# An attention-and-convolution kernel: where the first strip's projection, its normalization and the transposes stand in the order of work

## The chip, the cores and the metric

The kernel runs on one core of a Trainium2 chip. The metric is the device time of one execution in microseconds (us); lower is better. The shown time is the median of three executions. A profile is taken of one further execution, and all durations of single instructions come from that one.

Engines are named as the profile names them: PE is TensorE (matrix products; PEld is its weight load), DVE is VectorE, ACT is ScalarE, POOL is GpSimd, and SP is SyncE, whose queue issues the strip transfers. A line such as L62 is a line of the kernel's file.

## The reference

The input x has 8 images of 384 channels and 64 x 64 pixels, in float32. Two layers are applied, each on a group-normalized input and each with a residual:

```python
x = x + attention(_gn(x))      # layer 0
x = x + conv_layer(_gn(x))     # layer 1
```

- `_gn` normalizes 32 groups of 12 channels over all pixels of an image.
- Layer 0 is a LayerNorm over the channels, a q, k, v product, attention in windows of 8 x 8 pixels, and an output projection (`out @ proj_w + proj_b`). Half of the channels (4 heads of 48) use plain windows, the other half (4 heads) windows shifted by 4 pixels, with a mask. Each window's softmax has a relative position bias.
- Layer 1 is a 1x1 product with `w_in`, a filter in the 8 x 8 Fourier domain (`rfft2`, a product, `irfft2`), a depthwise 3x3 convolution, a gate (`gelu(x1) * x2`), and a 1x1 product with `w_out`.

## The kernel before, in words

**Tiles.** An image is cut into 8 strips of 8 rows, that is 512 tokens with 3 x 128 channels. A strip s of image b has two attention units, one for the plain and one for the shifted windows (br = 0 and 1), numbered w = 16b + 2s + br. Layer 1 of image b needs the group mean and deviation of the whole of layer 0's result x1, so it runs beside the attention of image b+1. It begins with strip 0 at place 16(b+1) + 2; before that come two units in which the attention of the new image has little of layer 1 beside it. The second of them, unit 16(b+1) + 1, is called the short unit here. It runs on PE from the end of one score product (pS) to the first q tile of the next unit.

**One unit on PE.** pS (scores), three tiles of pq (q and k of the next unit, 6 passes each), two tiles of pvv (v), pT (transposes of the softmax weights, `turn`), pA (weights times v, `apply`), and pr (output projection of a finished strip, `project`, three tiles of three passes). The pieces of layer 1 lie between: pt (`mix`), pf (`transform`), pz (`back`) and pw (`finish`).

**The other engines.** DVE does the softmax (e, mx, rc), the residual addition x_add after pr (L624), the statistics of the strip (st, in `keep`), eight of the nine taps of the convolution (zz, L784), and the LayerNorm scaling y. ACT copies q, k, v out of PSUM (qab, kab, kcd, qcd, v), takes exponentials, copies the transposes (eT) and the weighted values (o, L598 to L604), applies the second group norm (xn, `normal_x1`, L653) and copies z from pz. POOL does three copies of y (L451 to L453) and issues the transfers that put o into the layout oT for the projection. The oT of strip 0 has one buffer of its own, since that strip's projection can come only when the shifted windows of strip 7 have wrapped around.

**The second group norm.** `keep` takes the statistics of each strip of x1. When all eight are there, `second_mean` aggregates them (mv_b), PE averages over the groups (pm_b), DVE works out the variance (gs_b, gt_b), PE averages again (pv_b), and `second_std` takes the root on ACT (sd_b) and, on DVE, the reciprocal and the shift (sh, L638 to L645). `normal_x1` of strip 0 needs sh.

**What sets the order.** Each piece is put in a plan by `at(place, piece, ...)` (from about L843 on), where the place is a unit with a fraction. The pieces are issued in order of place. PE's instructions keep exactly this order. For the other engines a scheduler sets the order when the program is built; once built, each engine runs its own list in order. Strip transfers go through SP's queue, each behind a copy of q (`in_dense_work`); five buffers of tag "x" hold strips. PSUM has four "gemm" buffers of one bank and two "att" pairs.

**Empty instructions.** EMPTY (L29 to L33) lists how many empty instructions go between the dense products of each unit. They shift where the borders of PE's instruction blocks of 256 fall.

**The head.** Before the first unit the q, k and v weights are scaled by the LayerNorm's gain, and the mean over channels is taken off them (`centre` on ACT and PE, `take_off` on DVE, tile pc). The biases come from the tile pb. DVE also takes the statistics of the first image. Strip 0 is then normalized, its row sums `ln_sums` and the spread `rs_first` give the scale of y, and the first pq can start.

Of the kernel before, what the change touches and what calls it, by code (L numbers as in the profile page):

```python
# [18 lines left out]
NS = SW // WS  # L19
# [6 lines left out]
C_ID, C_ONES, C_GRP, C_FWD, C_INV, C_MASK = 0, 128, 256, 384, 512, 640  # L26
C_PICK = C_MASK + 3 * 64
N_CONST = C_PICK + 2
EMPTY = (128, 0, 0, 96, 52, 0, 0, 98, 11, 124, 11, 124, 3, 124, 11, 124, 11, 45, 43, 124, 52, 123, 11, 124,  # L29
         11, 124, 11, 124, 3, 124, 11, 124, 11, 45, 43, 124, 52, 123, 11, 124, 11, 124, 11, 124, 3, 124, 11, 124,  # L30
         11, 45, 43, 124, 52, 123, 11, 124, 11, 124, 11, 124, 3, 124, 11, 124, 11, 45, 43, 124, 52, 123, 11, 124,
         11, 124, 11, 124, 3, 124, 11, 124, 11, 45, 43, 124, 52, 123, 11, 124, 11, 124, 11, 124, 3, 124, 11, 124,
         11, 45, 43, 124, 52, 123, 11, 124, 11, 124, 11, 124, 11, 0, 0, 115)  # L33

STATS_AT = 2.16, 4.16, 5.16, 6.16, 7.16, 8.16, 9.16, 10.16

# [2 lines left out]
def block_kernel(ctx: ExitStack, tc: tile.TileContext, out, x, consts, fsel, wqk, wv, bqk, bv,  # L39
                 wp, bp, lng, lnb, rpb1, rpb2, w_in, w_dw, w_out, filt):  # L40
    nc = tc.nc
# [8 lines left out]
    def psum(name):  # L50
        return ps.tile([P, ST], F32, tag="gemm", name=name)

    def psum2(name):

        return ps.tile([P, 2, ST], F32, tag="att", bufs=2, name=name)
# [16 lines left out]
    def strip(tag, bufs, name):  # L72
        return sb.tile([P, KC, ST], F32, tag=tag, bufs=bufs, name=name)
# [72 lines left out]
    for j, to, n, t, hp, of in blocks:  # L146
        nc.gpsimd.dma_start(out=bqk_sb[to:to + n].rearrange("p (b j) -> p b j", b=2)[:, :, j],
                            in_=bqk[of:of + n, 4 * t:4 * t + 4].rearrange("p (b i) -> p b i", b=2)[:, :, hp])
# [19 lines left out]
    for br, tab in ((0, rpb1), (1, rpb2)):  # L168
        raw = sb.tile([P, 2, 64], F32, tag="t2", bufs=3, name=f"rpb_raw{br}")
        raw_bias.append(raw)  # L170
        for h in range(4):
            half = slice(h % 2 * 64, h % 2 * 64 + 64)
            for y2 in range(WS):
                nc.gpsimd.dma_start(
                    out=raw[half, h // 2, y2 * WS:(y2 + 1) * WS],
                    in_=bass.AP(tab.tensor, h * 225 + y2 * 15, [[15, 8], [1, 8], [1, 8]]),
# [25 lines left out]
    means, biases = {}, {}  # L202

    def all_biases():
        if not biases:
            biases["all"] = psum("pb")
        return biases["all"]

    def centre(w, *key):
        for k in range(KC):  # L210
            nc.scalar.activation(w[:, k], w[:, k], AF.Copy, scale=lng_sb[:, k:k + 1])
        pc = psum("pc")
        for k in range(KC):
            matmul(pc[:, 0:C], ones_c, w[:, k], start=(k == 0), stop=(k == KC - 1))
        means[key] = w, pc
# [83 lines left out]
    def at(place, piece, *args):  # L299
        plan.append((place, len(plan), piece, args))  # L300

    xs, ys, y2s, qks, vs, os_, ots, x1s, zs = ({} for _ in range(9))
# [10 lines left out]
    gs0, gs1, st0s, st1s, x1d = ({} for _ in range(5))  # L313
# [9 lines left out]
    def in_dense_work(i):  # L323


        if zs.get("gate"):
            behind(i, zs["gate"], mybir.DependencyClass.Sync, "transfer in dense work")
# [4 lines left out]
    def load(b, s, what):  # L332

        if b == 0 and (what == "stats" or what == "norm" and s < 3):
            xs[b, s, what] = first_x[s]
            return
        if what == "mix" and s == 0:
            xs[b, s, what] = xs.pop((b, s, "add"))
            return
        t = xs[b, s, what] = strip("x", 5, f"x_{what}_{b}_{s}")  # L340
        src = x1d[b][s] if what in ("mix", "finish") else rows_of(x[b], s)
        in_dense_work(nc.sync.dma_start(out=t, in_=src))
# [289 lines left out]
        strip_stats(st1s[b], s, xs[b, s, "add"])  # L632

    def store(b, s):
        in_dense_work(nc.sync.dma_start(out=x1d[b][s], in_=xs[b, s, "add"] if s == 0 else xs.pop((b, s, "add"))))


    def second_mean(b):  # L638
# [208 lines left out]
    for b in range(B):  # L847
        first = 2 * NS * b

        for s in range(NS):  # L850
            u = first - 16 + STATS_AT[s] if b else -10 + 0.1 * s
            at(u, load, b, s, "stats")
            at(u + (0.5 if b else 0.05), input_stats, b, s)
        if b == 0:

            at(-9.99, pack_qk, 0)
            at(-9.98, qk_weights, 0)
            at(-9.97, v_weights)
            at(-9.96, pack_qk, 1)
            at(-9.95, qk_weights, 1)  # L860
            for place, key in ((-9.82, ("qk", 0)), (-9.62, ("v",)), (-9.42, ("qk", 1))):
                at(place, take_off, *key)
            at(-9.26, qk_bias, 0)
            at(-9.26, v_bias)
            at(-9.26, qk_bias, 1)
            at(-2.7, spread_first)
            at(-0.6, position_bias, 0)
            at(-0.4, position_bias, 1)
            at(0.2, out_bias)
            at(0.2, filter_weights)  # L870
        at(first - 4.8 if b else -8, input_mean, b)
        at(first - 4.4 if b else -7.9, input_std, b)
        for s in range(NS):
            u = first + 2 * s

            v = u - 4
            early = 1.75 if b == 0 and s == 1 else 0
            at(v - 0.84 - early, load, b, s, "norm")
            at(v + 0.15 - early, group_normal, b, s)
            at(v + 0.45 - (1.35 if early else 0), ln_square, b, s)  # L880
            if b:
                at(v + 0.985, small_tiles, v + 1)
            at(v + 0.99 - early, ln_sums, b, s)
            at(v + 0.99 if (b, s) != (0, 1) else -2.6, ln_row, b, s)
            at(v + 1.35, ln_scale, b, s)

            if s:
                at(v + 1.50, shifted_half, b, s - 1, 1)
            else:
                at(u - 1.15, shifted_half, b, NS - 1, 1)  # L890
            at(u - 1.2 if s < NS - 1 else v + 1.55, shifted_half, b, s, 0)
            for br in range(2):
                w = u + br
                for t in range(3):
                    at(w - 1 + (0.14, 0.34, 0.55)[t], qk_tile, b, s, br, t)
                for g in range(2):
                    at(w - 1 + ((0.78, 0.86), (0.67, 0.88))[br][g], v_tile, b, s, br, g)
                at(w + 0.05, scores, b, s, br)
                at(w + 0.12, weights, b, s, br)

                at(w + 0.13, exponent, b, s, br)
                at(w + (0.23, 0.26)[br], divide, b, s, br)
                at(w + 0.80, turn, b, s, br)
                at(w + 1.00, apply, b, s, br)
                at(w + 1.07, put, b, s, br)

            if 0 < s < NS - 1:
                places = [u + 3 + f for f in (0.27, 0.45, 0.70)]
            else:
                places = [first + 2 * NS + f + (0.0 if s else 0.24) for f in (0.36, 0.44, 0.52)]  # L910
            at(int(places[0]) - 0.84, load, b, s, "add")
            for m in range(KC):
                at(places[m], project, b, s, m)
            at(places[2] + 0.1, keep, b, s)
            at(int(places[2]) + 1.15, store, b, s)
        first += 2 * NS
        at(first + 1.25, second_mean, b)
        at(first + (1.90 if b < B - 1 else 1.995), second_std, b)
        if b == B - 1:
            at(first + 2, tap_matrices)  # L920
        for s in range(NS):
            u = first + 2 + 2 * s
            at(u - 0.84, load, b, s, "mix")
            at(u + 0.02, normal_x1, b, s)
            for i in range(4):
                at(u + (0.28, 0.45, 0.60, 0.78)[i], mix, b, s, i)
            for j in range(2):
                at(u + (0.995, 1.02)[j], transform, b, s, j)
            if b < B - 1:
                at(u + 1.985, small_tiles, u + 2)  # L930
            at(u + 1.99, back, b, s)
            at(u + 2.08 if b < B - 1 or s < NS - 1 else u + 1.991, borders, b, s)

            for n, m in enumerate((0, 2, 1)):
                for tap in range(1, 6):
                    at(u + (2.62, 3.10, 3.5)[n] + 0.05 * tap + (0.4 if n == 2 and tap > 3 else 0), conv, b, s, m, tap)
                for tap in range(6, 9):
                    at(u + 4.2 + 0.25 * (n * 3 + tap - 6) / 9, conv, b, s, m, tap)
            if (b, s) in on_pool:
                for place, taps in ((2.45, (0, 1)), (2.8, (2, 3)), (3.15, (4, 5)), (4.15, (6, 7)), (4.3, (8,))):  # L940
                    at(u + place, pool_taps, b, s, taps)
            if (b, s) in on_pe:
                at(u + 2.3, conv_taps, b, s)
            at(u + 5.16, load, b, s, "finish")
            at(u + 4.5, gate, b, s)
            at(u + 6.10, finish, b, s)
# [5 lines left out]
    order = [p[2:] for p in sorted(plan, key=lambda p: p[:2])]  # L952
    dense, empty, counts = [], [0] * len(order), list(EMPTY)
    for i, (piece, args) in enumerate(order):
# [116 lines left out]
```

## Time and profile before

| what | value |
|---|---|
| median of 3 executions | 3534.93 us (3534.86 to 3538.03) |
| profiled execution | 3543.4 us |
| its span | 3541.2 us |
| PE busy | 3460.2 us, 98% |
| DVE busy | 3058.8 us, 86% |
| ACT busy | 2538.1 us, 72% |
| POOL busy | 1060.4 us, 30% |
| short unit at the change from image 2 to 3 (from 1230.53 us) | 23.31 us, PE busy 21.45 |
| long unit before it (1190.84 to 1230.53 us) | 39.69 us |
| long unit, stretch of 1191.00 to 1230.53 us: PE, DVE, ACT busy | 39.53, 31.20, 19.26 us |

The share of busy time says which engine has the least idle time over the whole run. The timeline gives start and duration of each group of instructions, and in brackets the idle time of the engine before it with what ended it ("issue" means that nothing which the profile shows was waited for). The waits view adds these brackets up over the run.

### The profile page before, as it was taken

How to read it: one execution, taken by the hardware profiler on the slowest of the kernel's cores; microseconds unless marked ns; L12 is line 12 of the kernel's file. 1: busy time of each engine (PE TensorE's matmuls, PEld its weight loads, DVE VectorE, ACT ScalarE, POOL GpSimd, SP SyncE). 2: the span in 40 equal slices, each digit the busy share in tenths (PEclk: the TensorE clock that was granted, in tenths of full speed). 3: DMA queues.
4: the chain of work that ended last, by engine and by line, in shares of the span. 5: the costliest groups of instructions: out<-in, count | busy, mean ns of one | idle time of the engine just before them, and what ended most of it. 6: DMA issues, size and time to landing. Idle time of an engine off the chain costs nothing.

```text
span 3541.2 us, 93350 instructions
## 1 busy us (share of the span) xinstructions
PE 3460.2 (98%) x36454; PEld 2197.0 (62%) x36454; DVE 3058.8 (86%) x4330; ACT 2538.1 (72%) x4069; POOL 1060.4 (30%) x1688
## 2 busy tenths in 40 slices
PE   7999999999999999999999999999999999999898
PEld 5665666656666666666666666666666666666454
DVE  4766589989998899988999889998899988987987
ACT  4877687768777687776777767777677767776474
POOL 5333223223232233222233223232233223221254
PEclk8999999999999999999999999999999999999999
DMA  4343234333433234333334323433234333323422
GB/s 125 98 143 106 81 107 156 108 107 122 138 130 127 98 110 156 130 106 118 125 128 144 121 89 134 144 112 136 99 118 154 115 107 110 105 99 108 155 108 81
DMA packets 176100, 421.12 MB, mean 119 GB/s; under 512 B 26656, under 2 KB 29243, under 8 KB 175688
## 3 DMA queue, kind: packets, MB, share of 16 engines
q1 hardware_dynamic: 138832, 364.25, 29.5%
q0 software_dynamic: 36416, 50.65, 5.1%
q8 instruction: 315, 5.16, 0.6%
q14 instruction: 97, 0.79, 0.1%
q10 hardware_dynamic: 440, 0.27, 0.0%
HBM read 263.92 MB, written 100.79 MB: 103 GB/s over the span
## 4 chain that ended last, share of the span: by engine, by line
PE 86%; DVE 8%; ACT 2%; DMA 2%; issue 1%; POOL 0%; SPq 0%; ACTq 0%; POOLq 0%; DVEq 0%
PE pq L62 26%; PE pr L62 14%; PE pvv L62 13%; PE pt L62 11%; PE pw L62 6%; PE pz L62 3%; PE pA L62 3%; PE pT L70 3%; PE pS L62 3%; DVE zz L784 2%; PE pf L62 2%; PE ln L62 1%; DVE acc L784 1%; DMA x_norm<-in_x_dram 1%; DVE t L680 1%
## 5 line engine op out<-in xcount | busy, mean ns | idle before, releaser
L784 DVE SCALAR_TENSOR_TENSOR zz<-z,dw_sb,zz 128x512 f32<-128x512 f32 x1331 | 1025.8, 797 | 10.8
L62 PE MATMUL pq<-y,wqk_sb 128*128 128x512 f32 x2160 | 992.7, 598 | 1.6 <-DVE y L437 0.8
L614 POOL DMA_DIRECT2D oT<-o x960 | 482.0, 509 | 964.4 <-ACT z L717 431.3
L62 PEld LDWEIGHTS pq<-y,wqk_sb 128*128 128x128 f32 x2160 | 404.3, 190 | 450.9 <-issue 409.8
L62 PE MATMUL pt<-wi_sb,xn 128*128 128x384 f32 x1536 | 535.3, 487 | 3.0 <-ACT xn L653 3.0
L62 PE MATMUL pr<-oT,wp_sb 128*128 128x512 f32 x1152 | 523.9, 593 | 2.0 <-DMA oT<-o 2.0
L62 PE MATMUL pvv<-wv_sb,y 128*128 128x192 f32 x2880 | 507.4, 326 | 0.0
L62 PEld LDWEIGHTS pvv<-wv_sb,y 128*128 128x128 f32 x2880 | 471.7, 190 | 48.7 <-issue 33.7
L62 PEld LDWEIGHTS pt<-wi_sb,xn 128*128 128x128 f32 x1536 | 290.9, 191 | 233.1 <-issue 78.0
L451 POOL COPY y<-y 128x384 f32<-128x384 f32 x112 | 86.3, 771 | 1114.6 <-PE pvv L62 645.1
L62 PEld LDWEIGHTS pr<-oT,wp_sb 128*128 128x128 f32 x1152 | 217.5, 190 | 264.2 <-issue 247.3
L469 ACT ACTIVATE kcd<-pq,bqk_sb 32x512 f32<-32x512 f32 x512 | 348.9, 681 | 8.9
L469 ACT ACTIVATE qab<-pq,bq_sb,cst 96x512 f32<-96x512 f32 (+1 forms) x256 | 197.9, 773 | 181.9 <-PE pq L62 179.5
L502 ACT COPY v<-pvv 128x384 f32<-128x384 f32 x256 | 121.6, 475 | 190.4 <-PE pvv L62 189.1
L469 ACT ACTIVATE kab<-pq,bqk_sb 96x512 f32<-96x512 f32 (+1 forms) x256 | 174.3, 681 | 93.0 <-PE pq L62 89.3
L469 ACT ACTIVATE qcd<-pq,bq_sb,cst 96x512 f32<-96x512 f32 (+1 forms) x256 | 197.6, 772 | 33.0 <-PE pq L62 27.5
L381 POOL TENSOR_TENSOR sq<-sq 128x512 f32<-128x512 f32 x122 | 204.8, 1679 | 5.8
L536 DVE TENSOR_TENSOR e<-e,mx 128x1024 f32<-128x1024 f32 x128 | 199.9, 1562 | 3.9
L529 DVE TENSOR_TENSOR e<-pS,bias 128x512 f32<-128x512 f32 (+2 forms) x200 | 108.2, 547 | 93.0 <-PE pS L62 93.0
L546 DVE TENSOR_REDUCE rc<-e 128x16 f32<-128x1024 f32 x128 | 155.1, 1212 | 35.2 <-ACT e L541 35.2
L62 PE MATMUL pw<-zz,wo_sb 128*128 128x512 f32 x496 | 182.8, 511 | 0.0
L624 DVE SCALAR_TENSOR_TENSOR x_add<-pr,vec,x_add 128x512 f32<-128x512 f32 x192 | 142.6, 743 | 39.6 <-PE pr L62 39.0
(163 smaller groups left out, 5382.8 us busy)
## 6 DMA issues: line engine op xcount, KB each, us to landing
x_add<-in_x_dram SPq DMA_DIRECT2D x64, 768.0 KB
x1d<-x_add SPq DMA_DIRECT2D x64, 768.0 KB
x_finish<-x1d SPq DMA_DIRECT2D x64, 768.0 KB
out_dram<-x_finish SPq DMA_DIRECT2D x64, 768.0 KB
x_norm<-in_x_dram SPq DMA_DIRECT2D x61, 768.0 KB
x_stats<-in_x_dram SPq DMA_DIRECT2D x56, 768.0 KB
x_mix<-x1d SPq DMA_DIRECT2D x56, 768.0 KB
oT<-o POOLq DMA_DIRECT2D x192, 96.0 KB, 3.8
```

The source lines that it names most:

```text
L62: tc.keep_in_program_order(nc.tensor.matmul(*args, **kw))
L70: tc.keep_in_program_order(nc.tensor.transpose(*args, **kw))
L381: nc.gpsimd.tensor_tensor(sq[:, 0, :], sq[:, 0, :], sq[:, k, :], ALU.add)
L451: nc.gpsimd.tensor_copy(dst[:, :, :, :, 0:4], src[:, :, :, :, 4:8])
L469: return nc.scalar.activation(dst[to:to + n], pq[of:of + n], AF.Identity, bias=bias[of:of + n], scale=scale)
L502: nc.scalar.copy(v[:, 384 * g:384 * (g + 1)], pvv[:, 0:384])
L529: nc.vector.tensor_tensor(e5[:, odd, :, a:z, :], pS[:, odd, :, a:z, :], bias_t[br, kind, odd].unsqueeze(2).to_broadcast([P, 2, z - a, 64]) ...
L536: zs["soft"] = nc.vector.tensor_tensor(e, e, mx.unsqueeze(2).to_broadcast([P, 2 * NS, 64]), ALU.subtract)
L546: nc.vector.tensor_reduce(rc, e, AX.X, ALU.add)
L614: nc.gpsimd.dma_start(out=oT[to % P:to % P + z - a, to // P, rows], in_=o[row + a:row + z, h // 2, of:of + n])
L624: after_softmax(nc.vector.scalar_tensor_tensor(t[:, m, :], pr, bp_sb[:, m:m + 1], t[:, m, :], ALU.add, ALU.add))
L784: i = nc.vector.scalar_tensor_tensor(acc.rearrange("p (r c) -> p r c", c=SW), z[:, dy:dy + 8, dx:dx + SW], dw_sb[:, m, TAPS[tap]:TAPS[tap] ...
```

## The change

The change has four parts.

1. **Output projection of strip 0.** The three `project` pieces of strip 0 of image b move from the unit 16(b+1) (places +0.60, +0.68, +0.76) to +1.115, +1.12, +1.125, right after pS of the short unit and before its first q tile. With them move the residual addition, the statistics (`keep`), the load of x_add and the store of the strip (a unit later each). `second_mean` moves from +1.25 to +1.50, which in PE's order is from after the first q tile to after the second. The store of strip 0 now takes x_add out of the table, and the normalization still uses the same buffer.
2. **Normalization of strip 0** (`normal_x1`) moves from +0.02 to +0.12, and the load ahead of it from -0.84 to -0.3.
3. **Transposes.** In odd units after w = 17, `turn` moves from 0.80 to 0.95: pT stands behind both v tiles in place of between them.
4. **The head.** The channel means of the second q,k weights get their own half of a pair buffer (`psum2("pb")`), so that their subtraction (`take_off`) and all three biases can come later, behind the reciprocal for strip 0. The row sums of strip 1 (`ln_sums`) come after `rs_first` in place of before.

The counts in EMPTY are changed too: 7177 empty instructions before, 7160 after.

```diff
-EMPTY = (128, 0, 0, 96, 52, 0, 0, 98, 11, 124, 11, 124, 3, 124, 11, 124, 11, 45, 43, 124, 52, 123, 11, 124,
...
+EMPTY = (129, 0, 0, 98, 53, 0, 0, 100, 11, 124, 11, 124, 3, 124, 11, 124, 11, 83, 6, 124, 53, 123, 11, 124,
...
-            biases["all"] = psum("pb")
+            both = psum2("pb")
+            biases["all"], biases["pc"] = both[:, 0], both[:, 1]
...
-        pc = psum("pc")
+        pc = biases["pc"] if key == ("qk", 1) else psum("pc")
...
-            xs[b, s, what] = xs.pop((b, s, "add"))
+            xs[b, s, what] = xs[b, s, "add"]
...
-        in_dense_work(nc.sync.dma_start(out=x1d[b][s], in_=xs[b, s, "add"] if s == 0 else xs.pop((b, s, "add"))))
+        in_dense_work(nc.sync.dma_start(out=x1d[b][s], in_=xs.pop((b, s, "add"))))
...
-            for place, key in ((-9.82, ("qk", 0)), (-9.62, ("v",)), (-9.42, ("qk", 1))):
+            for place, key in ((-9.82, ("qk", 0)), (-9.62, ("v",)), (-2.9, ("qk", 1))):
                 at(place, take_off, *key)
-            at(-9.26, qk_bias, 0)
-            at(-9.26, v_bias)
-            at(-9.26, qk_bias, 1)
+            at(-2.64, qk_bias, 0)
+            at(-2.58, v_bias)
+            at(-2.58, qk_bias, 1)
             at(-2.7, spread_first)
...
-            at(v + 0.99 - early, ln_sums, b, s)
+            at(v + 0.99 if (b, s) != (0, 1) else -2.69, ln_sums, b, s)
...
-                at(w + 0.80, turn, b, s, br)
+                at(w + (0.95 if br and w > 2 * NS + 1 else 0.80), turn, b, s, br)
...
+            elif s:
+                places = [first + 2 * NS + f for f in (0.36, 0.44, 0.52)]
             else:
-                places = [first + 2 * NS + f + (0.0 if s else 0.24) for f in (0.36, 0.44, 0.52)]
+                places = [first + 2 * NS + f for f in (1.115, 1.12, 1.125)]
...
-        at(first + 1.25, second_mean, b)
+        at(first + 1.50, second_mean, b)
...
-            at(u - 0.84, load, b, s, "mix")
-            at(u + 0.02, normal_x1, b, s)
+            at(u - (0.84 if s else 0.3), load, b, s, "mix")
+            at(u + (0.02 if s else 0.12), normal_x1, b, s)
```

## The prediction, made before the result

> **What bounds the kernel now.** I read the page's first and fourth parts, then the waits, then the timeline around one image change. TensorE (PE) does nearly everything, and the chain that ended last is mostly PE:
>
> ```profile
> PE 3460.2 (98%) x36454; PEld 2197.0 (62%) x36454; DVE 3058.8 (86%) x4330; ACT 2538.1 (72%) x4069; POOL 1060.4 (30%) x1688
> PE 86%; DVE 8%; ACT 2%; DMA 2%; issue 1%; POOL 0%; SPq 0%; ACTq 0%; POOLq 0%; DVEq 0%
> ```
>
> Only idle time of PE can be won, and there is little of it: outside the head (the first 54 us) the gaps over 0.25 us in PE's timeline add up to 51 us, some 26 in the tail (after 3298 us) and 23 at the image changes. Three waits of PE repeat there (total us, times, longest):
>
> ```profile
> PE pw L62 <- ACT o L604: 11.4, 13, 1.2
> PE pA L62 <- issue: 6.1, 6, 1.6
> PE pT L70 <- DVE e L548: 4.7, 6, 1.1
> ```
>
> One change, with T = 1230.53 for the end of the scores pS, where the short unit starts (start, duration; the bracket is idle time before):
>
> ```profile
> 1230.53 2.84 PE L62 MATMUL pq<-y,wqk_sb 128*128 128x512 f32 x6
> 1233.21 0.28 PE L62 MATMUL pm_b<-mv_b,cst 128*128 128x1 f32 x2
> ...
> 1247.17 0.85 PE L62 MATMUL pA<-eT,v 64*64 64x64 f32 x41 [1.17 <-issue]
> ...
> 1250.56 0.66 PE L62 MATMUL pw<-g,wo_sb 64*64 64x256 f32 x8 [0.69 <-ACT o L604]
> ```
>
> The next q tile starts at 1253.84, so the unit takes 23.31 us, with 1.86 idle. pm_b, the group mean, does not wait: the aggregate mv_b that it reads was ready ten microseconds earlier, in the long unit.
>
> ```profile
> 1219.40 0.75 DVE L624 SCALAR_TENSOR_TENSOR x_add<-pr,vec,x_add 128x512 f32<-128x512 f32 x1 [3.05 <-PE pr L62]
> ...
> 1223.49 0.81 DVE L266 BATCH_NORM_AGGREGATE mv_b<-st 128x2 f32<-128x144 f32 x1
> ...
> 1232.58 1.22 DVE L533 TENSOR_REDUCE mx<-e 128x16 f32<-128x1024 f32 x1
> ...
> 1240.62 1.75 DVE L437 TENSOR_TENSOR y<-y,rs 128x1536 f32<-128x1536 f32 x1
> ```
>
> **Image change: the moved projection.** Nine passes of pr for strip 0 leave the long unit, where PE never waits, and stand right after pS. They take 7.72 us (three tiles of 2.57) in either place, so this alone is worth nothing. What matters is what follows them. The three residual additions and three statistics of the strip go onto DVE inside the softmax of the short unit, mv_b needs the last of them, and pm_b stands in PE's program after the second q tile.
>
> PE reaches pm_b at T + 7.72 + 2 x 2.57 = T+12.9. DVE reaches mv_b later. The order in the changed program from mx on is one run without holes; start-to-start steps from the timeline: mx 1.13, three x_add at 0.66, subtraction 1.14, three statistics at 0.60, sum 1.24, reciprocal 0.29, product 1.14, four convolution taps zz at 0.66, y 1.67. That is 13.0 us; mx starts at T+2.05, so mv_b starts at T+15.1 and ends at T+15.9. The exponential (ACT, 1.06 us) ends about T+6.1, while DVE is still busy to T+6.2, so it adds no wait. With 0.15 us to PE (in the head mv_a ends 41.32, pm_a starts 41.46), pm_b runs at T+16.0: **PE stalls 3.1 us**. Behind it in PE's program stand the third q tile, both v tiles, pT, pz and pA; PE has nothing else to do. Hence the stall shifts the rest of the unit, unless that rest was waiting for something else. It was waiting for ACT, and ACT is shifted with it:
>
> ```profile
> 1242.22 1.02 ACT L558 COPY eT<-pT 128x1024 f32<-128x1024 f32 x1
> ...
> 1244.05 1.28 ACT L282 ACT_TABLE_LOAD   x1
> ...
> 1246.68 2.23 ACT L653 ACTIVATE xn<-x_add,sh,gs_b 128x512 f32<-128x512 f32 x3
> ```
>
> From the start of the first v tile (1238.58) to the last halves of pw (1250.56) are 11.98 us now. In the changed order: both v tiles 3.9 us on PE, then on ACT the second v copy 0.48, table 1.30, sd_b 0.2, eT 1.0, one xn 0.74, three z 1.75, two xn 1.48, the four o copies 1.16: 12.0. So even if the issue gap ahead of pA (1.17 here, 6.1 in six) goes, pw waits that much longer for o. Short unit: +3.0.
>
> The issue gap does probably go: it comes where four strip transfers (1235 to 1244.5 us, near 400 GB/s) run beside the instruction queue's, and one of the four, the store of strip 0, moves a unit later. The Trainium skill ("Runtime: NRT & Kernel Launch", Instruction fetch mechanics) says that TensorE's instructions are streamed in blocks of 256, and that crossing a border is mostly hidden. The trace has six gaps of 0.62 to 1.56 us, which is not hidden. By the rule none of the 6.1 us is to be had, by the rows all; o's chain makes both sums nearly alike.
>
> **Other moves there.** The loads of x_add and the store of strip 0 pass x_norm in SP's queue; x_norm then lands by about T+21.5, ahead of sh, so nothing waits. The oT buffer of strip 0 exists once, so POOL's nine oT transfers of the next image wait for pr's end at T+7.7 (they could start near T+2); 4.5 us of issue (the row shows nine in 4.49 us) ends before y's copies on POOL, due after y at T+14.8: nothing, unless the next reader of oT were near, and it is two units away. normal_x1's later place costs nothing by itself: its three activations are counted above.
>
> **Transposes last in odd units.** Two units on, at 1288.73, pT waits 0.72 for e, and pw 0.77 for o. With pT after both v tiles the first goes. But ACT then has v, two xn, v, xn, eT (xn waits for x_mix, landing 1291.0): eT ends at 1294.6 where pA began at 1293.49, and the last pw comes at 1297.6 instead of 1297.25: +0.35. In ordinary odd units eT ends some 0.8 us ahead of pA in either order: nothing (from -0.3 to +0.5 each if the cover fails).
>
> **First change and tail.** At 394 us there is no convolution: mv_b ends near T+13.6, stall 0.65, and the later eT costs about 0.9 in the next unit, less the 0.45 issue gap: +1.0. In the tail pm_b waits about 3.7 us more, but sh comes near 3343 against 3344.1 now; pt there waits 2.98 us for xn already: 0, from -1.5 to +1.5.
>
> **Head.** The take-off of the second q,k weights and the biases leave the way of the last statistics:
>
> ```profile
> 34.58 1.35 DVE L219 TENSOR_TENSOR wqk_sb<-wqk_sb,pc 128x1152 f32<-128x1152 f32 x1 [2.83 <-PE pc L62]
> ...
> 40.51 0.81 DVE L266 BATCH_NORM_AGGREGATE mv_a<-st 128x2 f32<-128x144 f32 x1
> ```
>
> Statistics resume at 31.75 instead of 35.85 (4.1) and skip 1.0 of biases: mv_a 5.1 earlier. The reciprocal ahead of rs_first follows (50.44 to 45.4; rs_first itself waited until 51.68 behind strip 1's sums, which now come after it). Those 48 passes (24 take 1.5 us at 44.7 us, about 3 us in all) then stand between rs_first and the first q tile:
>
> ```profile
> 51.68 1.79 PE L62 MATMUL rs_first<-lr,cst 128*128 128x128 f32 x8
> 54.25 8.11 PE L62 MATMUL pq<-y,wqk_sb 128*128 128x512 f32 x13 [0.78 <-DVE y L437]
> ```
>
> pq starts between 49 and 50.2: -4.1 to -5.3. The clock granted to PE was 0.50 from 52.0 to 58.8, so the first q passes took twice as long; another phase of it moves this by up to 2 us either way. I take -4.7, from -3 to -7.
>
> The Trainium skill ("TensorE: Matmul & The Clock Gate", Part 1) says that full speed comes after about 3.4 us of activity. By that, 48 more passes just ahead of pq could warm it: about 2 us more. The trace speaks for less, since the clock stayed at 0.50 through a similar burst at 44.7 to 48.6.
>
> The empty instructions (7177 to 7160) keep the block borders at the same index in each image: nothing.
>
> **Sum** against the profiled execution (3543.4 us, span 3541.2 and 2.2 around it): -4.7 + 1.0 + 6 x (3.0 + 0.35) = +16.4, thus 3559.8. The median of three runs, 3534.93, lies 8.5 below the profiled one, so I forecast 3534.93 + 16.4 = 3551, slower by 0.46%. This kernel's measurement can tell about 0.2% (7 us) from no change.
>
> **Rivals.**
> (a) The gaps of PE vanish and the time falls. This needs mv_b by T+13, three microseconds earlier than my chain, and o early too. For it: the long unit on PE is 39.5 us against 31.2 of DVE work, so DVE has room to enter the short unit ahead. Against: mx needs pS, which fixes T. Per change 1.02 (issue), half of pw's 0.85 and 0.7 (pT): about 2.2, with the head -4.7 - 13 = -18: 3517; with the head's -7 and all of pw's, 3510. Chance 0.25.
> (b) Only the stall is missing, and o's chain stays as I have it: -4.7 + 1.0 + 6 x 0.35 = -2, 3533; the same results if the stall is there and is won back two units later. Chance 0.20.
> (c) My forecast, 3545 to 3558: 0.42.
> (d) The stall, and sh late as well: should x_norm land after T+24.6, its three y operations and two sums (2.9 us) delay sh, then xn, o and pw: 1 to 2 us more per change, 3558 to 3566. For it: DVE waits 1.06 us for x_norm in this unit now. Chance 0.13.
> (e) That the change does not do what it says has no room: the order is fixed in the program. Only the border's gap could stay; o's chain hides it.
>
> Range 3517 to 3562. Faster 0.25, within 0.2% 0.20, slower 0.55.
>
> **What would show it.** In the changed profile: a wait "pm_b <- DVE mv_b" of about 3 us, six times, 19 in all; the short unit (end of pS to its next q tile) near 34 us where 23.3 + 7.7 = 31.0 would be even; pw still waiting for o; no issue gap at pA; mv_a near 35.4 and the first q tile near 49.5. I am wrong if pm_b hardly waits, or if pw waits for o much less than 1 us.

## The result and the profile after

The changed kernel takes 3558.5 us (median of 6 runs, 3557.8 to 3566.5) against 3538.79 for the kernel before (6 runs, 3534.86 to 3542.08). The ratio is 1.0058, with a 95% interval of 1.0048 to 1.0068: slower by 0.6%. The forecast was 3551 with a range of 3517 to 3562. The profiled execution took 3557.8 us with a span of 3556.0, which is 14.8 more than the span before; the forecast sum was +16.4. By the medians of six runs the difference is 19.7: the profiled execution of the kernel before (3543.4 us) was slower than all six of its runs. (In the text above the two totals of empty instructions are exchanged: 7160 stand in the kernel before, 7177 in the changed one.)

The first part of the page after hardly differs, and its chain of waits breaks off after about a quarter of the span, so it is not used:

```profile
PE 3468.9 (98%) x36454; PEld 2202.1 (62%) x36454; DVE 3042.3 (86%) x4330; ACT 2537.4 (71%) x4069; POOL 1051.2 (30%) x1688
```

PE's busy time grew by 8.7 us for the same number of products. Some of the loss is thus not idle time: the same products ran longer. The waits view of PE after (total us, times, longest):

```profile
PE pm_b L62 <- DVE mv_b L267: 18.4, 8, 3.6
...
PE pw L62 <- ACT o L605: 12.2, 7, 1.8
...
PE pA L62 <- ACT eT L559: 6.2, 7, 1.6
...
PE pT L70 <- DVE e L549: 1.1, 1, 1.1
```

The first line is new and is the wait that was forecast (19 us at six changes). Of its 18.4 us, 14.7 stand at the six later image changes, 3.6 in the tail and 0.2 at the first change. pT's waits and the issue gap at pA are gone, and pA waits for eT in their place. The timeline of PE after, at the change shown before; T is now 1217.74, the end of pS:

```profile
1233.26 0.38 PE L62 MATMUL pm_b<-mv_b,cst 128*128 128x1 f32 x2 [2.45 <-DVE mv_b L267]
...
1243.27 1.16 PE L62 MATMUL pA<-eT,v 64*64 64x64 f32 x64
...
1248.05 0.66 PE L62 MATMUL pw<-g,wo_sb 64*64 64x256 f32 x8 [1.82 <-ACT o L605]
1248.65 4.54 PE L62 MATMUL pw<-zz,wo_sb 128*128 128x512 f32 x8
1253.03 2.74 PE L62 MATMUL pq<-y,wqk_sb 128*128 128x512 f32 x6
```

The short unit takes 1253.03 - 1217.74 = 35.3 us, where 31.0 would have been even and 34 was forecast. The last 1.7 us stand in the line of pw<-zz: eight passes take 4.54 us, where they took 2.85 before. Nothing is waited for in between; each pass is simply longer. The view by windows shows why (columns: length, PE busy, PEld, DVE, ACT, POOL, granted clock, DMA share, GB/s):

```profile
1244.00:1248.00 4.00, 2.23 (x104) 1.35 (x93) 1.29 (x2) 4.00 (x11) 0.00 (x0) 1.00 0.02 4
...
1249.00:1252.00 3.00, 3.00 (x4) 1.02 (x4) 0.69 (x1) 1.86 (x2) 3.00 (x7) 0.50 0.30 82
1252.00:1253.00 1.00, 1.00 (x5) 0.84 (x4) 0.68 (x1) 0.00 (x0) 1.00 (x3) 0.88 0.22 61
1253.00:1256.00 3.00, 3.00 (x9) 1.41 (x9) 2.75 (x4) 0.92 (x2) 2.83 (x3) 1.00 0.39 136
```

Behind this wait of PE the granted clock is 0.50 for 3.4 us, and 1.71 us of work are lost. Read in windows of 1 us, the trace of before has no such stretch between 80 and 3345 us. The trace after has nine at the six later image changes, five behind pm_b's wait and four behind pw's. Three of the six short units have both, and take 37.0 us.

DVE after, at the same change:

```profile
1230.07 1.75 DVE L438 TENSOR_TENSOR y<-y,rs 128x1536 f32<-128x1536 f32 x1
1231.74 0.74 DVE L785 SCALAR_TENSOR_TENSOR zz<-z,dw_sb,zz 128x512 f32<-128x512 f32 x1
1232.40 0.80 DVE L267 BATCH_NORM_AGGREGATE mv_b<-st 128x2 f32<-128x144 f32 x1
```

mv_b ends at T+15.5; the working gave T+15.9. The offset of the changed kernel at matching points of the two traces (ends of pS) gives the balance by stage:

| stage | forecast | measured |
|---|---|---|
| head, to 330 us | -4.7 | -8.1 |
| first image change | +1.0 | -0.9 |
| six later image changes | +20.1 | +26.6 (3.8, 3.2, 5.0, 4.7, 3.9, 6.0) |
| tail | 0 | -2.9 |
| sum | +16.4 | +14.8 |

The 26.6 us come out of the gaps of PE in the two timelines: pm_b's waits 6 x 2.45 = 14.7; nine half-clock stretches 15.4; pw's wait in the short unit 5.9 more (11.0 against 5.1); pA's wait for eT two units later 5.6; less the issue gaps 6.1, pT's waits 3.6 and pw's waits two units later 5.1. Together that is +26.8.

### The profile page after: what moved, and what is told of

The parts are those of the page before. It is cut to its first block, busy times and chain, and to the rows that moved or that the text cites. A ratio compares the mean times of both kernels' runs of the same rounds, so it can differ in the third digit from the quotient of the medians.

```text
span 3556.0 us, 93336 instructions
## 1 busy us (share of the span) xinstructions
PE 3468.9 (98%) x36454; PEld 2202.1 (62%) x36454; DVE 3042.3 (86%) x4330; ACT 2537.4 (71%) x4069; POOL 1051.2 (30%) x1688
## 5 line engine op out<-in xcount | busy, mean ns | idle before, releaser
L62 PE MATMUL pvv<-wv_sb,y 128*128 128x192 f32 x2880 | 498.5, 326 | 0.0
L542 ACT ACTIVATE e<-e 128x1024 f32<-128x1024 f32 x128 | 135.2, 1056 | 58.0 <-DVE e L537 56.2
```

What stands on the lines that cost most here:

```text
L62: tc.keep_in_program_order(nc.tensor.matmul(*args, **kw))
L542: nc.scalar.activation(e, e, AF.Exp)
```

## The experiments

My theory after the result: the loss is pm_b's wait and the half clock that waits bring; the head is a gain. The rivals are named with each run. Where only the six later changes count, the number is the difference of offsets in the profiled run. Where an edit altered the number of PE's instructions, EMPTY was adjusted so that the block borders stay within a few instructions of the same place in each image. The experiments ran on three chips. Each ratio is to the kernel before on the same chip (medians 3541.19, 3538.17 and 3537.12 us), so medians of runs that stand under different chips can differ by some 3 us for that alone: the first four ran on the first chip, the next four on the second, the last two on the third.

**PE kept busy through the wait.** Before pm_b, for b = 1 to 6, three products on constants go into the tile that pm_b overwrites.

```diff
+        if name in [f"b{i}" for i in range(1, B - 1)]:
+            for _ in range(3):
+                matmul(pm, grp, wp_sb.rearrange("p k c -> p (k c)")[:, 0:ST], start=True, stop=True)
         matmul(pm[:, 0:1], grp, mv[:, 0:1], start=True, stop=True)
```

> The changed kernel, but PE runs three idle products (six passes of 0.43 us, on constants, into the tile that pm_b then overwrites) ahead of pm_b at the six image changes b = 1 to 6, where PE waited 2.45 us for mv_b. No result changes. Theory (the clock): the wait of 2.45 us is followed by a stretch of 3.4 us at granted clock 0.50 in five of the six changes, worth 1.71 us each. With PE kept busy through the wait, these five stretches go; the products take 2.57 us where 2.45 were idle, so 6 x 0.12 - 5 x 1.71 = -7.8 us against the changed kernel's 3558.5: about 3550.7. Rival (the wait alone costs; the half clock comes from something else): the stretches stay, +0.7 us or no change.

Measured: 3553.2 us, 1.0031 of before (1.0020 to 1.0042); the changed kernel had 1.0058. The five stretches behind pm_b are gone, though PE still gets no further for the 2.45 us:

```profile
1228.25 2.74 PE L62 MATMUL pm_b<-wp_sb,cst 128*128 128x512 f32 x6
1230.87 0.38 PE L62 MATMUL pm_b<-mv_b,cst 128*128 128x1 f32 x2
```

So idle PE, not the place of pm_b, halves the clock. In this trace the six changes lose 18.1 us in place of 26.6, near theory's -7.8. Of the four stretches behind pw one is left, and one has come behind a wait of pA of 2.71 us. Part of the gain is given back: pA's wait for eT two units later is 9.1 us over six changes, against 5.6.

**The group mean later.**

```diff
-        at(first + 1.50, second_mean, b)
+        at(first + 1.80, second_mean, b)
```

> The changed kernel, with second_mean at place 1.80 for 1.50: pm_b stands between the two v tiles in place of after the second q tile, 4.5 us later on PE. The scheduler then puts three more convolution taps (2.0 us) ahead of mv_b, which so ends near T+17.4, about when PE gets there. Theory (pm_b's stall and its clock are the loss): the wait shrinks from 2.45 to at most 0.5 us and the half-clock stretches behind it go: 6 x (-2.45 to -1.95) - 5 x 1.71 = -20 to -23 us against the changed kernel: 3535 to 3538, level with the kernel before. Rival (o's chain on ACT sets the unit's end, whatever pm_b does): the wait moves to pw <- o in whole or in half, -3 to -10 us.

Measured: 3537.82 us, 0.9989 (0.9980 to 0.9997): 20.7 us below the changed kernel's median, and 0.7% by the two ratios. pm_b waits 0.46 us at each change, and two half-clock stretches are left at the image changes. In the trace the six changes lose 6.8 us in place of 26.6: three quarters of their loss hang on the place of one small product and on the convolution taps that move with it.

**The new head alone.** The diff is part 4 of the change.

> The kernel before with the new head alone (take-off of the second q,k weights, biases and row sums of strip 1 later). Theory: the trace of the changed kernel is 8.1 us ahead from the second unit on, 4.8 of it because the first q tile starts earlier and 3.4 because PE comes to full clock before the first q passes and loses no stretch at 75 to 80 us; all of it is kept to the end: -8 us against the kernel before (3538.8): about 3530.7. Rival (the clock's part depends on the phase of a window that runs by itself): only -4.8, about 3534.

Measured: 3530.08 us, 0.9970 (0.9958 to 0.9981), 11 us better. The trace is 11.5 us ahead after the second unit. That number varies from execution to execution: eight profiled runs with the new head were 8.1 to 11.5 us ahead there, four with the old one between 2.7 ahead and 0.3 behind. On average the new head is worth 8.6 us. The six image changes neither gain nor lose here (0.0 us), though the issue gap ahead of pA is gone: pw's wait for o, 1.79 us, has taken its place.

**The moved projection alone**, with its loads, store and second_mean, old head, transposes in the old place.

> The kernel before with the moved projection of strip 0 alone (with its loads, store, statistics, second_mean at 1.50 and normalization at 0.12), old head, transposes in the old place. Theory: the loss is here. In the changed kernel's trace six image changes lose 26.7 us, and the later transposes took part in that only two units on (0.92 us on average at pA, against 1.57 for pT and pw before); so about +26.7 + 4 - 0.9 - 2.9 = +27 us against the kernel before: 3565, slower than the changed kernel by the head's 8. Rival (the later transposes lose in the short unit as well, by eT's late copy): +15 to +20, 3554 to 3559.

Measured: 3563.63 us, 1.0065 (1.0051 to 1.0079). The six changes lose 27.7 us in the trace, with eleven half-clock stretches. The median is 22 us above the kernel before on the same chip (3541.19), between the two expectations. The trace leans to theory, whose sum has 30.7 us for the six changes, where the rival's has some 19 to 24. The rest is the head, which was 2.7 us ahead in this execution though unchanged, and the tail, 3.2 ahead. The direct test is the run "The changed kernel with the transposes in the old place" below.

**The later transposes alone** (part 3 of the change).

> The kernel before with the later transposes of odd units alone. Theory (my step: worth about nothing in ordinary odd units, and at the image changes pT's wait of 0.72 and pw's of 0.57 to 1.04 two units on are exchanged for a wait of pA for eT of 0.6 to 1.65, as the changed kernel's trace has it): between -3 and +4 us against the kernel before, by trace at most +0.5 per image change. Rival (transposes last are a gain wherever PE waits for the softmax): the 4.7 us of pT's waits go and nothing comes, -5 us.

Measured: 3551.39 us, 1.0040 (1.0027 to 1.0053): 13 us slower (8.9 us at the six changes in the trace), and neither expectation held. The short unit's own transposes belong to the odd units as well, which my step had passed over. There the issue gap and pw's wait (1.9 us, in two pieces) become one wait of 2.4 us:

```profile
1253.78 1.08 PE L62 MATMUL pw<-g,wo_sb 64*64 64x256 f32 x8 [2.42 <-ACT o L604]
1254.79 4.07 PE L62 MATMUL pw<-zz,wo_sb 128*128 128x512 f32 x8
```

Behind each of the six there is a half-clock stretch (10.2 us in all); before had none.

**The o copies first.** In the kernel with second_mean at 1.80, pw still waits 1.82 us for o, behind two of the activations xn on ACT. Here xn of strip 0 is held behind the o copies.

```diff
-            nc.scalar.activation(by_window(xn[:, k, :]), image_order(t[:, k, :]), AF.Identity,
+            i = nc.scalar.activation(by_window(xn[:, k, :]), image_order(t[:, k, :]), AF.Identity,
...
+            if s == 0:
+                after_out(i)
```

> The changed kernel with second_mean at 1.80 as before, and the three activations xn of strip 0 held behind the o copies of the short unit on ACT. Theory (o's chain on ACT is the next thing that sets the unit's end): pw waits 1.82 us for o at six changes, and xn is not read until about 6 us later; with the 2.2 us of xn out of the way the wait goes, 6 x -1.8 and the half-clock stretches that followed it: about -11 to -14 us against the same kernel without this (3537.8): 3524 to 3527. Rival (xn is then late for pt): a wait of pt for xn takes its place and nothing is won.

Measured: 3529.35 us, 0.9974 (0.9964 to 0.9983). That is 8.5 us below the kernel without it by the medians, but these are of two chips; by the ratios it is 0.15%, some 5 us, and the intervals overlap a little. In the traces the six changes lose 1.0 us in place of 6.8. The six waits for o are gone. Some of it is lost again two units on:

```profile
1281.30 1.52 ACT L654 ACTIVATE xn<-x_mix,sh,gs_b 128x512 f32<-128x512 f32 x2 [2.06 <-DMA x_mix<-x1d]
1282.72 0.46 ACT L503 COPY v<-pvv 128x384 f32<-128x384 f32 x1
1283.08 0.82 ACT L654 ACTIVATE xn<-x_mix,sh,gs_b 128x512 f32<-128x512 f32 x1
1283.80 0.99 ACT L559 COPY eT<-pT 128x1024 f32<-128x1024 f32 x1
```

With the transposes last, eT stands on ACT behind three xn, and these wait for the load of x_mix. PE comes earlier, the load does not, and pA waits 3.03 us:

```profile
1284.84 1.38 PE L62 MATMUL pA<-eT,v 64*64 64x64 f32 x64 [3.03 <-ACT eT L559]
```

**The same, with the transposes in the old place.**

> As the last one, with the transposes in the old place. Theory: pA's waits for eT two units on (0.6 to 2.3 us, 9.1 over six changes in the run with second_mean at 1.80) go, pT's wait for e (0.7) and pw's for o (0.4 to 1.0) return: -1 to -4 us against the last kernel. Rival: no difference, the two orders lose the same.

(The waits of pA in that run add up to 9.7, not 9.1.)

Measured: 3517.06 us, 0.9942 (0.9928 to 0.9955): 12 us better than the last one, three times what was expected. eT now stands ahead of two of the xn, pA waits nowhere, and no half-clock stretch is left between 60 and 3289 us; the last run had four. My size left the clock out once more.

**The new head and the o copies first**, projection and transposes as before.

> The kernel before with the new head, and xn of strip 0 held behind the o copies (place of normalization 0.10 for that), the projection and the transposes where they were. In the run with the new head alone pw waited 1.79 us for o at six changes and the issue gap ahead of pA was gone. Theory (o's chain sets the end of the short unit in the old order too): the 1.79 us go, 6 x -1.79 = -10.7 us against the head alone (3530.1): about 3519.5; if the issue gap comes back (1.0 on average), 3525. Rival (the moved projection is needed to use that room): no gain, 3530.

Measured: 3521.33 us, 0.9953 (0.9940 to 0.9965). The waits for o in the short unit go, and the issue gap at pA comes back at some changes (0.34 to 0.73 us), as feared. In the trace the six changes are 13.6 us shorter than with the head alone. The intervals of this and the last run overlap: whether the projection's new place is itself worth anything stays open.

**The changed kernel with the transposes in the old place.**

> The changed kernel with the transposes in the old place; all else of it kept (second_mean at 1.50). The later transposes alone cost the kernel before 13 us, and 12 us in the kernel with second_mean at 1.80. Theory (they cost mostly through the half clock that a long wait for o brings; in the changed kernel the wait at pm_b and the next one at pw bring it already): little is won here, the six changes of the moved projection alone lost 27.7 us against 26.7 in the changed kernel: 3555 to 3560. Rival (the cost is additive): 3558.5 - 10 to 13 = about 3547.

Measured: 3557.57 us, 1.0061 (1.0047 to 1.0075), the same as the changed kernel. In the traces the six changes lose 25.9 us here and 26.6 there, so in this change the later transposes cost next to nothing, where they cost 8.9 alone. So costs do not add. It is not pm_b's wait that has brought pw's half clock already: both traces have five stretches behind pm_b and four others behind pw. It is pw's own wait, which with the moved projection is one piece in either order (2.05 us here, 1.82 with the later transposes), with no issue gap left to merge with:

```profile
1248.27 0.66 PE L62 MATMUL pw<-g,wo_sb 64*64 64x256 f32 x8 [2.05 <-ACT o L605]
```

**PE kept busy through the transposes' wait.** As in the first experiment, with the three products ahead of pw's first ones in the short unit, in the kernel with the later transposes alone.

> The kernel before with the later transposes alone, and three idle products (six passes of 0.43 us on constants, into a pw tile that is then overwritten) ahead of pw's first products in the short unit of the six changes, where PE waited 2.42 us for o. No result changes. Theory (the clock): in that run each such wait was followed by 3.4 us at clock 0.50; with PE kept busy all six stretches go: 6 x (0.15 - 1.71) = -9.4 us against the later transposes alone (3551.4): about 3542. Rival (the wait alone): +0.9 or no change.

Measured: 3552.25 us, 1.0038 (1.0024 to 1.0051), no gain, as the rival said. But the trace speaks against the rival's reason: all six stretches in the short unit are gone, and that unit is 1.6 us shorter at the change looked at. The gain is lost two units on, where pA waits 1.4 to 3.2 us for eT at five changes instead of 0.58, again behind xn and the load of x_mix. At each of the five, pA's wait is 1.0 us more than that of xn for x_mix (0.40 to 2.14 us):

```profile
1292.55 1.52 ACT L653 ACTIVATE xn<-x_mix,sh,gs_b 128x512 f32<-128x512 f32 x2 [0.40 <-DMA x_mix<-x1d]
```

The clock is a real cost, but removing it paid nothing here, since the load of x_mix was due next.

## Why the prediction was right, and where not

- **pm_b's stall** (3.1 us a change): right in place and mechanism, 2.45 measured. mv_b came at T+15.5 instead of T+15.9, and PE reached pm_b at T+13.1 instead of T+12.9. The late mean (20.7 us back) confirms it as the main cause. In the tail the forecast wait of 3.7 us came as 3.56.
- **o's chain makes the unit's end, so the issue gap's going wins nothing**: right. The issue gap went and pw's wait grew from 0.69 to 1.82 us. From the first v tile to the last halves of pw it was 11.9 us, forecast 12.0. In the run with the head alone the issue gap went too, and pw waited 1.79. That the later store of strip 0 takes the issue gap away is not shown: with the store in its old place the gap was gone at all six changes with the head alone, and at five with the transposes alone. Nor did any run test whether it comes from an instruction block's border.
- **The half clock was missing from the sum.** The working used the clock gate for the head alone. It cost 15.4 us at the six changes and is why they lost 26.6 and not 20.1. The difference is smaller than that because the stall was 3.9 us shorter in all, and because the gaps two units on shrank by 3.1 us where the sum had +2.1.
- **Transposes last, +0.35 a change**: wrong as a part by itself. The step looked at the unit two further on and left out the short unit. There the two gaps merge into one of 2.4 us, which halves the clock. Inside this change it cost next to nothing (26.6 against 25.9 us at the six changes), since pw's wait was one piece without it.
- **Head, -4.7**: the first q tile was forecast between 49 and 50.2 and came at 49.49, as worked out. The rest, to -8.1, is the clock: it was 0.94 on average from 50 to 56 us, where it had been 0.50 from 52.0 to 58.8, and a stretch of before at 75.9 to 79.3 us is gone.

```profile
49.49 8.60 PE L62 MATMUL pq<-y,wqk_sb 128*128 128x512 f32 x18
...
50.00:56.00 6.00, 6.00 (x14) 2.60 (x13) 1.97 (x7) 4.55 (x8) 6.00 (x28) 0.94 0.25 50
```

  The estimate from the Trainium skill ("TensorE: Matmul & The Clock Gate", Part 1), about 2 us more by a warmer clock, had the right sign; the sum took nothing for it. The experiments' traces agree: in the eight with the new head the clock is full from 0.6 us before to 1.4 us after the start of the first q tile, in the four with the old head only 4.6 to 5.0 us after it.
- **First change and tail** (+1.0 and 0): -0.9 and -2.9. At the first change pm_b waited 0.2 us and not 0.65, and a wait of 0.69 for kcd is gone. The tail's part was not tested; its half-clock stretches lie differently in every run.
- **The rivals.** Neither (a) nor (b) came: the stall was there. The time of 3558.5 lies at the edge of (d), but (d) is not what happened: x_norm's five operations end at 1241.0 us in the changed trace, before sd_b, on which sh then waits, so x_norm does not delay sh. (The 3510 in (a) is a slip; its own terms give 3512.5.)

The errors of the terms had both signs and partly cancelled: the sum of 16.4 against 14.8 looks better than its parts, and that is in part luck.

## What to carry to other kernels

When a reduction's last input moves next to its consumer on a busy engine, work out both arrival times in the programs' order; moving the consumer a few products later costs one constant and here gave back 20.7 us. A wait of TensorE of about two microseconds can cost a half-clock stretch besides; whether it does hung here on how it fell on the clock's grid (next section). Expect the costs of parts not to add. When one engine is made earlier, look for the next transfer that does not become earlier with it.

## What the runs showed of the hardware

The clock gate answers to shorter gaps than I had thought, and to where they fall. In every trace the granted clock changes only at points of a grid with steps of 3.413 us, and the grid lies differently in each execution. Between 300 and 3286 us of the twelve traces, 34 steps had 1.89 us or more in which PE was idle, and the clock was 0.50 in the step behind every one of them. Of 19 steps with 1.78 to 1.89 us idle, 11 were followed by such a stretch; of those with less, none. A stretch is thus one step of the grid, 3.4 us, and cost 1.71. Two waits at pm_b of the same 2.45 us in the changed kernel show it. The first two lines hold the first wait, the third the second wait, and the fourth is the step behind it (columns as above; PE's idle time is the length less PE busy):

```profile
1228.35:1231.77 3.41, 2.45 (x6) 0.76 (x4) 3.41 (x5) 2.99 (x5) 0.54 (x2) 1.00 0.60 196
1231.77:1235.18 3.41, 1.92 (x6) 1.09 (x7) 3.27 (x10) 1.88 (x3) 2.00 (x3) 1.00 0.97 308
...
1658.43:1661.85 3.41, 0.96 (x4) 0.15 (x2) 3.41 (x5) 3.01 (x5) 1.67 (x4) 1.00 0.82 244
1661.85:1665.26 3.41, 3.41 (x6) 1.68 (x7) 3.20 (x9) 0.26 (x1) 0.48 (x1) 0.50 1.00 382
```

The grid splits the first wait into 0.96 and 1.49 us, and the clock stays at 1.00 (up to 1238.59 us, through the step behind as well). The second lies in one step, and the next runs at 0.50. So the length of a gap alone does not decide.

In the three runs with second_mean at 1.50 and no filling, a single gap of 2.45 us was followed by a half-clock stretch 15 times in 18. A gap of 2.1 to 2.4 us (transposes alone): 6 in 6. A single one of 1.8 us (first three experiments), 4 times in 18. A gap of 1.8 to 2.1 us some 15 us behind one of 2.45: 14 in 18. The longest, 3.16 us at a pA of the last experiment, fell half and half (1.60 and 1.56) and was followed by none. The gaps at the image changes of before, all under 1.6 us, never. The Trainium skill ("TensorE: Matmul & The Clock Gate", Part 1) gives about 3.4 us of idleness for the fall; the runs show that 1.9 us of it within one step are enough.
